# All values of thirteen pooled token tiles behind the routed experts, in four layouts of the pooled keys, and the residual loaded after the last tile

## The chip, the cores and the metric

The kernel runs on one core of a Trainium2 chip. The metric is the time of one execution in device microseconds (us); lower is better. A profiled execution also gives a span, from its first to its last instruction, which the views below are measured against.

## What is computed

The reference takes 2048 tokens of 512 numbers through two residual layers. Each layer normalises its input, computes a mixing branch `s` and a feed-forward branch, and adds `s * silu(ffn)` to the input:

```
xn = layernorm(x)
x  = x + rwkv(xn) * silu(moe2(xn))          # layer 0
xn = layernorm(x)
s  = attention(xn; 16 heads, 4 key heads)   # layer 1
g  = silu(shared_experts(xn) + routed_experts(xn))
x  = x + s * g
```

The change lies in layer 1. Its attention is over a short list of keys. The first 1792 tokens are pooled in blocks of 64 to 28 keys; only the last 256 tokens stay as single keys. A query sees a key if the key's position is not after its own. So a tile of 128 tokens, number `i` of 16, sees at most `2 * (i + 1)` pooled keys; tiles 0 to 13 see nothing but pooled keys, and tiles 14 and 15 are computed apart. The probabilities of one tile are 128 tokens x 16 heads x the keys, and the attention's result is their product with the values, multiplied by the output weights.

The feed-forward branch has two shared experts, which all tokens pass, and sixteen routed ones. Each token goes to four routed experts, weighted by a normalised gate.

## The kernel before

**Order of layer 1.** After the routing is known, the kernel computes keys and values, then tiles 14 and 15 of the attention (`full_group`), mixed with the shared experts of the last 512 tokens. It folds the query weights with the pooled keys into `sem` (lines 1515 to 1529), so that a tile's scores are one product with `xT`. The remaining shared experts follow (`hidden_shared`, line 972, and `down_shared`, line 1121); their result, with `acc`, is written by SP to two tables in main memory, `comb[0]` and `comb[1]`, one for each half of the 512 columns (line 1129).

**The routed loop.** Tokens are sorted by expert into tiles of 128 rows; there are 64 full ones' worth of rows and up to 80 tiles. `hidden_rows(j)` loads one expert's weights (line 674 to 678) and the tile's rows `x` (line 1674), turns the rows over (line 1681), and computes the hidden part (line 1688). `down_rows` computes the second product (line 1712), VectorE multiplies it with the gate (line 1717, four buffers of `y`), and GpSimd (POOL) sends it with an indirect transfer that adds each row to its token's row in both halves of `comb` (line 1720). Tiles from 65 on stand in a condition on the count of tiles; in the profiled execution 73 were needed, and seven conditions were passed by. An engine that passes one by still brings the semaphores to where they would have been.

**Attention inside the loop.** `attention()` is a generator. For each block of 256 tokens it projects the queries (two steps), computes scores and softmax of two tiles (`scores`, one step each, lines 1576 and 1582), and then, for tiles that are not in `LAST`, turns the probabilities over and multiplies them with the values (`turned` and `values`, lines 1608 and 1619). The loop takes a step every two tiles or so. A scheduler may place instructions ahead of where the program has them, when nothing holds them back; each engine then runs its own list strictly in order.

**Layouts of the pooled values.** With 32 keys for each head, four heads fill the 128 rows of a product, and a tile takes four products ("layouts" below). Tiles 1 to 7 see at most 16 keys. For these `vo8` holds the same values packed at 16 keys a head, and a tile takes two layouts. `vo8` is filled through main memory: `vo` is written to `vo_d` (line 1530), and SP loads 16 pieces of 16 rows from it (line 1534).

**The end.** The residual, `xr1`, was stored earlier. Its loads, `xo`, eight of 512 KB, are issued by SP inside the loop beside its last sixteen full tiles. After the loop `tiles.close()` gives the space of the weights, rows and `y` back. Then SP loads the sums from `comb` (line 1764, sixteen loads of 256 KB); PE computes the values of `LAST`, tiles 5 to 13; and `close` takes two tiles at a time: ScalarE's Silu on the sums (line 1772), VectorE's product with the attention's result (line 1774) and the addition of the residual (line 1778), and a store (line 1779). `pinned` keeps the Silus at their places in ScalarE's order: the first two stand behind the copy of tile 11's result.

Of the kernel before, what the change touches and what calls it, by code (L numbers as in the profile page):

```python
# [77 lines left out]
def tile_kernel(ctx: ExitStack, tc: tile.TileContext, a: dict):  # L78
# [1433 lines left out]
    vo8 = wq.tile([P, 2, D], F32, name="vo8")  # L1512
# [18 lines left out]
    for p in range(2):  # L1531
        for u in range(2):
            for j in range(4):
                nc.sync.dma_start(
                    out=vo8[(4 * u + j) * NARROW : (4 * u + j + 1) * NARROW, p, :],
                    in_=vo_d[j * KP : j * KP + NARROW, 2 * p + u, :],
                )

# [11 lines left out]
    fin = ctx.enter_context(tc.tile_pool(name="fin", bufs=NT // 2))  # L1550
# [6 lines left out]

    WIDE = NARROW * MB // P
    wide = [aq.tile([P, H, KP], F32, name=f"wide{i}") for i in range(WIDE, FULL[0])]
    near = [aq.tile([P, H, NARROW], F32, name=f"near{i}") for i in range(3)]  # L1560
    for t_ in (*wide, *near):
        nc.gpsimd.memset(t_, 0.0)

    def room_of(i):

        if i == 0:
            return aq.tile([P, H, KP], F32, tag="t1", name="all_keys"), KP
        nk = (i + 1) * P // MB
        return (near[i % 3] if i < WIDE else wide[i - WIDE]), nk
# [28 lines left out]
    def turned(i):  # L1598
# [3 lines left out]
        each = P // keys  # L1602
        nw = H // each
# [3 lines left out]
        for g in range(nw):  # L1607
            nc.tensor.transpose(
                pt[:, g, :], s[:, each * g : each * (g + 1), :].rearrange("p h k -> p (h k)"),
                ident,  # L1610
            )
        sT = aq2.tile([P, HKV, P], F32, tag="sT", name="sT")
        nc.scalar.copy(sT[:, 0:nw, :], pt)
        return i, nw, sT, vo if keys == KP else vo8
# [13 lines left out]
    LAST = range(5, FULL[0])  # L1628
# [106 lines left out]
    for j in range(NRT + 1):  # L1735

        with contextlib.ExitStack() as more:
# [9 lines left out]
            i = j - (FULL_TILES - NT)  # L1747
            if 0 <= i < NT and i % 2 == 0:
                xo = fin.tile([P, 2, D], F32, tag="xo", name="xo")
                nc.sync.dma_start(  # L1750
                    out=xo, in_=xr1[i * P : (i + 2) * P, :].rearrange("(n p) d -> p n d", p=P)
                )
                rest_of[i] = xo
# [3 lines left out]
    fin2 = ctx.enter_context(tc.tile_pool(name="fin2", bufs=NT // 2))  # L1757


    sums_of = {}  # L1760
    for i in range(0, NT, 2):
        y = fin2.tile([P, 2, D], F32, tag="y", name="y")
        for h, c_ in enumerate(comb):
            nc.sync.dma_start(
                out=y[:, :, h * D // 2 : (h + 1) * D // 2],
                in_=c_[i * P : (i + 2) * P, :].rearrange("(n p) d -> p n d", p=P),
            )
        sums_of[i] = y
# [123 lines left out]
```

## Time and profile before

| | |
|---|---|
| median of three runs | 1923.88 us (1922.08 to 1924.26) |
| profiled execution | time 1919.63 us, span 1917.9 us |
| last matmul of the shared experts ends | 1332.3 us |
| first product of the routed loop | 1340.29 us |
| first and last accumulating scatter start | 1347.20 and 1875.25 us |
| sums loaded from | 1883.65 us |
| VectorE's last stretch begins | 1895.27 us |

All times in the profile are microseconds from the start of the span. PE is TensorE's matmul, PEld its weight load, DVE VectorE, ACT ScalarE, POOL GpSimd, SP the engine that issues most transfers; SPq marks SP's issues. A line of the timeline has start, length, engine, source line, operation, output and inputs, and how many instructions were merged; in square brackets stands the idle time before it and what ended it. A line of the waits has who waited for whom, the total, how often, and the longest. The view by stretches gives, for a stretch of time, the busy time of each engine with its count, the granted clock of TensorE, the mean share of the 16 DMA engines and what they moved. A long share of busy time says that an engine was occupied, not that the end hangs on it.

### The profile page before, as it was taken

How to read it: one execution, taken by the hardware profiler on the slowest of the kernel's cores; microseconds unless marked ns; L12 is line 12 of the kernel's file. 1: busy time of each engine (PE TensorE's matmuls, PEld its weight loads, DVE VectorE, ACT ScalarE, POOL GpSimd, SP SyncE). 2: the span in 40 equal slices, each digit the busy share in tenths (PEclk: the TensorE clock that was granted, in tenths of full speed). 3: DMA queues.
4: the chain of work that ended last, by engine and by line, in shares of the span. 5: the costliest groups of instructions: out<-in, count | busy, mean ns of one | idle time of the engine just before them, and what ended most of it. 6: DMA issues, size and time to landing. Idle time of an engine off the chain costs nothing.

```text
span 1917.9 us, 23670 instructions
## 1 busy us (share of the span) xinstructions
PE 1848.1 (96%) x8107; PEld 1286.8 (67%) x8107; DVE 762.0 (40%) x1528; ACT 536.5 (28%) x1006; POOL 461.5 (24%) x349
## 2 busy tenths in 40 slices
PE   6999999999999999999989999999999999999996
PEld 4777777777877777777533654445767777777662
DVE  8354545272725435352166543421323223233313
ACT  6224232332423232332134112221222222222223
POOL 0211121120212111010210453000344444444341
PEclk9899999999999999999999999999999999999998
DMA  8657686635563434437461553122999999999896
GB/s 269 223 180 249 234 272 213 211 99 173 163 222 113 154 120 133 143 99 252 149 213 49 180 207 115 50 83 71 316 298 306 329 309 269 279 272 269 229 257 186
DMA packets 235989, 381.40 MB, mean 199 GB/s; under 512 B 19405, under 2 KB 136909, under 8 KB 234969
## 3 DMA queue, kind: packets, MB, share of 16 engines
q1 hardware_dynamic: 205784, 332.79, 52.3%
q0 software_dynamic: 28784, 45.63, 10.6%
q10 hardware_dynamic: 1296, 1.41, 0.3%
q8 instruction: 67, 1.10, 0.2%
q14 instruction: 58, 0.47, 0.1%
HBM read 294.04 MB, written 85.72 MB: 198 GB/s over the span
## 4 chain that ended last, share of the span: by engine, by line
PE 56%; DMA 6%; DVE 1%; issue 1%; ACT 1%; POOL 1%; SPq 0%; DVEq 0%; ACTq 0%; POOLq 0%
PE ph L1688 10%; PE py L1712 9%; PE pg L585 8%; PE py L607 4%; PE py L1121 4%; PE ph L972 3%; DMA comb<-y,to 3%; PE pq L1367 2%; PE proj L219 2%; PE po L727 2%; PE tp L1681 2%; PE ps L1576 1%; PE ps L1582 1%; PE pl L886 1%; PE pw L1492 1%
## 5 line engine op out<-in xcount | busy, mean ns | idle before, releaser
L585 PE MATMUL pg<-xg,w 128*128 128x256 f32 (+1 forms) x2304 | 494.9, 368 | 0.0
L585 PEld LDWEIGHTS pg<-xg,w 128*128 128x128 f32 x2304 | 419.5, 190 | 90.5 <-issue 42.3
L1720 POOL DMA_INDIRECT comb<-y,to x146 | 228.1, 1562 | 313.9 <-DMA comb<-y,to 183.4
L607 PE MATMUL py<-wd,hT 128*128 128x512 f32 x544 | 257.1, 593 | 3.5 <-DVE hT L592 3.5
L1688 PEld LDWEIGHTS ph<-xg,w 128*128 128x128 f32 (+1 forms) x1776 | 202.0, 182 | 40.4 <-ACT xg L1683 36.6
L1688 PE MATMUL ph<-xg,w 128*128 128x128 f32 (+1 forms) x1776 | 216.3, 278 | 0.7 <-issue 0.3
L592 DVE TENSOR_TENSOR hT<-sg,pg 128x256 f32<-128x256 f32 (+1 forms) x144 | 57.3, 402 | 380.4 <-ACT sg L590 380.2
L1712 PE MATMUL py<-w,ht 128*128 128x512 f32 (+1 forms) x438 | 207.8, 593 | 0.0
L590 ACT ACTIVATE sg<-pg 128x256 f32<-128x256 f32 (+1 forms) x144 | 53.0, 370 | 359.6 <-PE pg L585 359.3
L607 PEld LDWEIGHTS py<-wd,hT 128*128 128x128 f32 x544 | 102.2, 190 | 73.0 <-issue 61.9
L1717 DVE TENSOR_SCALAR y<-py,g 128x512 f32<-128x512 f32 x73 | 54.6, 748 | 219.7 <-PE py L1712 219.7
L958 ACT ACTIVATE ht<-ph,b1t 128x128 f32<-128x128 f32 (+1 forms) x222 | 81.2, 366 | 178.2 <-PE ph L1688 176.1
L1712 PEld LDWEIGHTS py<-w,ht 128*128 128x128 f32 (+1 forms) x438 | 75.9, 191 | 51.4 <-issue 45.2
L1683 ACT COPY xg<-tp 128x512 f32<-128x512 f32 x74 | 43.3, 585 | 186.9 <-PE tp L1681 186.9
L1121 PE MATMUL py<-w,hT 128*128 128x512 f32 (+1 forms) x192 | 89.4, 595 | 0.0
L972 PE MATMUL ph<-xT,w 128*128 128x512 f32 (+1 forms) x192 | 88.0, 597 | 0.0
L1059 POOL DMA_INDIRECT xs<-acc,slot x64 | 63.2, 987 | 66.0 <-DMA xs<-acc,slot 43.6
L267 POOL TENSOR_TENSOR ex<-st_p,qt 128x1024 f32<-128x1024 f32 x8 | 18.3, 2287 | 235.7 <-DVE qt L266 235.7
L727 PE MATMUL po<-wo,yb 128*128 128x512 f32 x128 | 57.4, 607 | 9.7 <-ACT acc L736 9.7
L1681 PEld LDWEIGHTS tp<-ident,x 128*128 128x128 f32 x296 | 36.9, 140 | 38.6 <-issue 20.8
L219 PE MATMUL proj<-xm,wr 128*128 128x256 f32 x256 | 61.5, 396 | 0.0
L219 PE MATMUL proj<-xm,wk 128*128 128x256 f32 x256 | 60.2, 389 | 0.0
(412 smaller groups left out, 2142.5 us busy)
## 6 DMA issues: line engine op xcount, KB each, us to landing
w<-in_w_dram SPq DMA_DIRECT2D x152, 352.0 KB
w<-in_w_dram SPq DMA_DIRECT2D x152, 256.0 KB
w<-in_w_gate_dram SPq DMA_DIRECT2D x72, 512.0 KB
w<-in_w_up_dram SPq DMA_DIRECT2D x72, 512.0 KB
wd<-in_w_down_dram SPq DMA_DIRECT2D x72, 512.0 KB
xs<-zero SPq DMA_DIRECT2D x16, 1360.0 KB
x<-xs SPq DMA_DIRECT2D x74, 272.0 KB
w<-in_w_dram SPq DMA_DIRECT2D x76, 192.0 KB
```

The source lines that it names most:

```text
L219: nc.tensor.matmul(out=ps[:, j, :], lhsT=w_[:, c, (o0 + j) * P : (o0 + j + 1) * P], rhs=xm[:, c, :], start=(c == 0), stop=(c == NC - 1),)
L585: nc.tensor.matmul(out=pg[:, i, 0:n], lhsT=w[:, c, i * FH + f * P : i * FH + (f + 1) * P], rhs=xg[:, c, 0:n], start=(c == 0), stop=(c == N ...
L607: nc.tensor.matmul(out=p, lhsT=hT[:, u * P : (u + 1) * P], rhs=wd[:, f, :], start=first_, stop=last_,)
L727: nc.tensor.matmul(out=po, lhsT=yb[:, c, s * P : (s + 1) * P], rhs=wo[:, c, :], start=(c == 0), stop=(c == NC - 1),)
L958: nc.scalar.activation(dst, src, AF.Relu, bias=b)
L972: nc.tensor.matmul(out=ph[0:n, :], lhsT=up(w, f, n, c), rhs=xT[:, c, cols], start=(c == 0), stop=(c == NC - 1),)
L1059: ins = nc.gpsimd.indirect_dma_start(out=xs, out_offset=bass.IndirectOffsetOnAxis(ap=slot[:, i, k : k + 1], axis=0), in_=acc[:, i, :], in_ ...
L1121: nc.tensor.matmul(out=py, lhsT=hT[0:n, e, f, s * P : (s + 1) * P], rhs=down(w, f, n), start=(e == 0 and f == 0), stop=(e == NS - 1 and f ...
L1681: nc.tensor.transpose(tp[:, c, :], x[:, c * P : (c + 1) * P], ident)
L1688: nc.tensor.matmul(out=ph[0:n, :], lhsT=up(w, f, n, c), rhs=xg[:, c, :], start=(c == 0), stop=(c == NC - 1),)
L1712: nc.tensor.matmul(out=py, lhsT=hT[0:n, f, :], rhs=down(w, f, n), start=(f == 0), stop=(f == NF1 - 1),)
L1720: nc.gpsimd.indirect_dma_start(out=c_, out_offset=bass.IndirectOffsetOnAxis(ap=to, axis=0), in_=y[:, h * D // 2 : (h + 1) * D // 2], in_of ...
```

## The change

- `LAST` grows from tiles 5 to 13 to tiles 1 to 13: only tile 0's values stay in the attention's steps. The steps in the loop go from 33 to 29.
- The values are packed at 8, 16, 24 and 32 keys for each head, and a tile takes the smallest that holds its keys: tiles 1 to 3 one layout of 128 rows, 4 to 7 two, 8 to 11 three, 12 and 13 four. Each tile 1 to 13 has its own buffer of probabilities, cleared by POOL (13 clears for 9).
- The packed values are loaded by ACT in fifty pieces of 8 to 24 rows, in place of SP's sixteen.
- The residual is loaded behind the loop in five loads (two of 512 KB, three of 1 MB), ahead of the sums; the sums come in ten loads in place of sixteen, of 256 or 512 KB each.
- The pairs of tiles are closed in the order of their numbers, pair 12 last.

```diff
-    vo8 = wq.tile([P, 2, D], F32, name="vo8")
+    by_keys = {k: wq.tile([P, H * k // P, D], F32, name=f"vo{k}") for k in (8, 16, 24)}
...
     nc.sync.dma_start(out=vo_d, in_=vo)
-    for p in range(2):
-        for u in range(2):
-            for j in range(4):
-                nc.sync.dma_start(
-                    out=vo8[(4 * u + j) * NARROW : (4 * u + j + 1) * NARROW, p, :],
-                    in_=vo_d[j * KP : j * KP + NARROW, 2 * p + u, :],
-                )
+    for k, rows_ in by_keys.items():
+        for h in range(H):
+            r0 = h * k
+            while r0 < (h + 1) * k:
+                r1 = min((h + 1) * k, r0 // P * P + P)
+                k0 = h % 4 * KP + r0 - h * k
+                nc.scalar.dma_start(
+                    out=rows_[r0 % P : r0 % P + r1 - r0, r0 // P, :],
+                    in_=vo_d[k0 : k0 + r1 - r0, h // 4, :],
+                )
+                r0 = r1
+    by_keys[KP] = vo
...
-    WIDE = NARROW * MB // P
-    wide = [aq.tile([P, H, KP], F32, name=f"wide{i}") for i in range(WIDE, FULL[0])]
-    near = [aq.tile([P, H, NARROW], F32, name=f"near{i}") for i in range(3)]
-    for t_ in (*wide, *near):
-        nc.gpsimd.memset(t_, 0.0)
+    probs = {}
+    for i in range(1, FULL[0]):
+        k = min(k for k in by_keys if k >= (i + 1) * P // MB)
+        probs[i] = aq.tile([P, H, k], F32, name=f"probs{i}")
+        nc.gpsimd.memset(probs[i], 0.0)
...
-        each = P // keys
-        nw = H // each
+        nw = H * keys // P
...
-    LAST = range(5, FULL[0])
+    LAST = range(1, FULL[0])
...
-            i = j - (FULL_TILES - NT)
-            if 0 <= i < NT and i % 2 == 0:
-                xo = fin.tile([P, 2, D], F32, tag="xo", name="xo")
-                nc.sync.dma_start(
-                    out=xo, in_=xr1[i * P : (i + 2) * P, :].rearrange("(n p) d -> p n d", p=P)
-                )
-                rest_of[i] = xo
...
     tiles.close()
-    fin2 = ctx.enter_context(tc.tile_pool(name="fin2", bufs=NT // 2))
+    fin = ctx.enter_context(tc.tile_pool(name="fin", bufs=1))
+    GROUPS = ((0, 2), (2, 2), (4, 4), (8, 4), (12, 4))
     sums_of = {}
-    for i in range(0, NT, 2):
-        y = fin2.tile([P, 2, D], F32, tag="y", name="y")
+    for i, n_ in GROUPS:
+        xo = fin.tile([P, n_, D], F32, name=f"xo{i}")
+        nc.sync.dma_start(
+            out=xo, in_=xr1[i * P : (i + n_) * P, :].rearrange("(n p) d -> p n d", p=P)
+        )
+        for k in range(0, n_, 2):
+            rest_of[i + k] = xo[:, k : k + 2, :]
+    for i, n_ in GROUPS:
+        y = fin.tile([P, n_, D], F32, name=f"y{i}")
         for h, c_ in enumerate(comb):
             nc.sync.dma_start(
                 out=y[:, :, h * D // 2 : (h + 1) * D // 2],
-                in_=c_[i * P : (i + 2) * P, :].rearrange("(n p) d -> p n d", p=P),
+                in_=c_[i * P : (i + n_) * P, :].rearrange("(n p) d -> p n d", p=P),
             )
-        sums_of[i] = y
+        for k in range(0, n_, 2):
+            sums_of[i + k] = y[:, k : k + 2, :]
...
-    closing = [i for i in range(0, NT, 2) if i < LAST[0] - 1]
-    closing += [i for i in (*range(0, NT, 2),) if i not in closing and i != FULL[0] - 2]
-    closing += [FULL[0] - 2]
+    closing = [i for i in range(0, NT, 2) if i != FULL[0] - 2] + [FULL[0] - 2]
```

More of the change, by code (lines that the diff above doesn't have):

```diff
@@ L1549, in tile_kernel @@
     aq2 = ctx.enter_context(tc.tile_pool(name="aq2", bufs=2))
-    fin = ctx.enter_context(tc.tile_pool(name="fin", bufs=NT // 2))
     tiles = ExitStack()
@@ L1567, in room_of @@
             return aq.tile([P, H, KP], F32, tag="t1", name="all_keys"), KP
-        nk = (i + 1) * P // MB
-        return (near[i % 3] if i < WIDE else wide[i - WIDE]), nk
+        return probs[i], (i + 1) * P // MB
     def scores(i, qg, u):
@@ L1608, in turned @@
             nc.tensor.transpose(
-                pt[:, g, :], s[:, each * g : each * (g + 1), :].rearrange("p h k -> p (h k)"),
-                ident,
+                pt[:, g, :], s.rearrange("p h k -> p (h k)")[:, g * P : (g + 1) * P], ident,
             )
@@ L1613, in turned @@
         nc.scalar.copy(sT[:, 0:nw, :], pt)
-        return i, nw, sT, vo if keys == KP else vo8
+        return i, nw, sT, by_keys[keys]
     def values(i, nw, sT, by_row):
```

## The prediction

> **What bounds the kernel now.** Start with the page: rows 1 and 2 give the engines' shares and the granted clock.
>
> ```profile
> PE 1848.1 (96%) x8107; PEld 1286.8 (67%) x8107; DVE 762.0 (40%) x1528; ACT 536.5 (28%) x1006; POOL 461.5 (24%) x349
> PE   6999999999999999999989999999999999999996
> PEclk9899999999999999999999999999999999999998
> DMA  8657686635563434437461553122999999999896
> ```
>
> TensorE is busy everywhere but at the two ends, at full clock. From slice 29 (1342 us), where the routed-expert loop begins, the DMA row is at 9 as well. So the change touches three stages with different limits: the shared experts (to 1332), the loop (1340 to 1867) and the end. The view by stretches separates them.
>
> ```profile
> 1340.00:1380.00 40.00, 39.47 (x217) 28.11 (x218) 10.86 (x30) 9.99 (x24) 12.61 (x9) 1.00 1.07 325
> 1380.00:1640.00 260.00, 259.85 (x1503) 192.04 (x1502) 74.65 (x254) 68.53 (x164) 114.66 (x74) 1.00 1.03 302
> 1640.00:1806.00 166.00, 165.97 (x906) 120.66 (x904) 55.28 (x164) 38.97 (x91) 66.30 (x43) 1.00 0.92 257
> 1806.00:1853.00 47.00, 47.00 (x271) 33.06 (x271) 10.79 (x43) 12.87 (x31) 19.05 (x12) 1.00 1.04 316
> 1857.00:1880.00 23.00, 18.59 (x70) 10.49 (x69) 0.75 (x1) 5.81 (x13) 12.40 (x8) 0.85 0.47 56
> ```
>
> After the length come the busy times of PE, PEld, DVE, ACT and POOL, then clock, DMA share, GB/s. PE is full in the loop, but so is something that no busy time shows: the accumulating scatters. For 1416 to 1640, the waits of POOL and the answer on line 1720 say:
>
> ```profile
> POOL comb L1720 <- DMA comb<-y,to: 110.8, 39, 6.7
> DMA to landing us min/median/max: 4.4/6.2/9.4
> ```
>
> Each tile adds its rows to both halves of `comb`, and a half's next scatter waits for the last to land. Tile 9's first scatter starts at 1416.58, tile 40's at 1636.82: 7.10 us a tile, nearly always ended by the landing of the one before. Two chains run abreast, PE's and this one. The end hangs on the second:
>
> ```profile
> SPq L1764 <- DMA comb<-y,to: 20.9, 1, 20.9
> L1737 POOLq INC_SWDGE_SEM x7: 847/857/891, 1875.3 to 1882.6; - x7
> 1883.65 9.90 SPq L1764 DMA_DIRECT2D y<-comb  x16
> 1892.88 1.28 ACT L1772 ACT_TABLE_LOAD   x1
> 1895.27 2.36 DVE L1774 TENSOR_TENSOR y<-xT,y 128x1024 f32<-128x1024 f32 x2 [34.17 <-DMA y<-comb]
> ```
>
> SP waits for the last scatter and for POOL's bookkeeping of seven skipped tiles behind it; the last tile's first scatter starts at 1873.40, and the sums are loaded from 1883.65. Call that moment T. Silu waits for ACT's turn (T+9.2), VectorE starts at T+11.6 and then never stops: 16 operations to 1913.52 (18.25 us), and the last store ends the span at 1917.9.
>
> **The change part by part.** Sums are against the profiled execution: span 1917.9, time 1919.63, which is 4.25 under the median of the three runs; I add the difference to the median.
>
> *Values out of the loop.* A wide tile of four layouts takes 3.87 us at the end (transposes at 1880.46 and 1884.34), 0.97 a layout. Before, tiles 1 to 4 cost two layouts each inside the loop: 8 x 0.97 = 7.8 us of PE. They go. The end had 3 x 2 + 6 x 4 = 30 layouts; it gets 3 x 1 + 4 x 2 + 4 x 3 + 2 x 4 = 31: +1.0 us of PE, which lies beside the loads at the end and costs nothing while these last longer (below).
>
> *Queries of the first block, ahead of the loop.* The built order puts the first block's 16 projections, both score tiles and tile 0's values before the first routed tile. SP's queue causes that: 16 loads of `vo8` (10.23 us from 1271.25 to 1281.48) no longer stand ahead of the cos/sin loads. PE work only moves (6.9 + 5.2 + 0.9 before line 1121's end, as 16 x 0.43, 4 x 0.86 + 4 x 0.43, and the small tile; PE was 100% busy in both places). But tile 0's values now wait for a copy between transposes and products: 0.58 us plus both hand-overs, about 0.9. And the first routed tile starts 13 us later, at about 1353.3 where it was 1340.29, so the first scatter goes from 1347.20 to about 1360.6.
>
> *Fifty loads on ACT.* They replace 16 on SP. Line 1534's issues have a median of 0.418 us, with the gap to the next 0.46; ACT's own constants at 1043 to 1044 go out at 0.4 to 0.5. So ACT issues for 50 x 0.46 = 23 us, behind it stand the four copies `wt`, `sem` and then every relu of the next shared block. The Trainium skill's "DMA: Bandwidth & Descriptors", section "Rules for kernel authors", speaks against it: coalesce many small transfers, "under 64 KB you're paying mostly overhead". These have 16 to 48 KB. If its section "Anatomy of one DMA" held with 2.0 us fixed for each in turn, it would be 100 us; the trace's 16 loads of 32 KB took 10.23 us together, so the pitch decides. I work ACT's end out: start 1271.3, 23 us of issue and 4.6 of copies would end at 1299, but the last four loads take semaphores used by the second block's cos/sin, whose buffer comes free only when VectorE has read the second projection (1305 + 0.7), plus 2.5 for that load: about 1310. PE has 6.9 us of shared hidden, 6.9 of projections and 6 of scores from 1291.1, to 1311, before it needs the first relu. Cost 0.4 us; bounds 0 and 10 (no cover at all from 1301 to 1311). POOL's 13 clears against 9 lie in an idle POOL.
>
> *Loop.* PE: -7.8 + 0.9 + 0.4 = -6.5. The scatters: until tile 12 the loop has almost no attention work, so tiles come at 5.8 us and DMA is full, as in the loop's first tiles, where the trace shows 7.8 us a scatter round (tile 1 at 1354.39, tile 9 at 1416.58). From 1360.6: 12 x 7.8 = 93.6, then 28 rounds at 7.1 and 22 at 6.9 (line 1720's median of 6.2 plus 0.7; 5.9 where less is moved) = 350.6: tile 62 at 1804.8. It was at 1806.43. The last ten rounds took 67.0 us to 1873.40 (no attention, DMA full, then empty) and will again. So T moves by 1804.8 - 1806.4 = -1.6 us, though PE has finished 6.5 earlier. Four buffers of `y` can hold the lag of some three tiles. Bounds: -6.5 (PE alone sets it) and +4 (7.2 a round in the middle).
>
> *The residual behind the loop.* Eight loads of 512 KB went out beside the last sixteen tiles, 4.2 MB hidden. Now five loads stand ahead of the sums on SP, in space that `tiles.close()` has to free: the built program puts the waits on all eight scatter semaphores on the first of them, and the first load of sums then has none left. They start at T, not earlier, and push the sums. The 16 sums took 15.0 us from 1883.65 to 1898.67 for the same 4.2 MB, at this rate in the middle:
>
> ```profile
> 1890.00:1894.00 4.00, 4.00 (x14) 2.04 (x13) 0.00 (x0) 1.70 (x2) 0.00 (x0) 1.00 1.09 358
> ```
>
> 4.19 MB at 358 GB/s are 11.7 us, so 3.3 is start and landing. The first pair's sum now lands at T + 3.3 + 11.7 + 1.5 = T+16.5. By the fit of "Anatomy of one DMA" (bytes at 436 GB/s) the residual would take 9.6, and the whole forecast would be 2.1 lower; the trace's 358 is taken. Behind the landing come the table load (1.28, now waiting for the sum) and one Silu (1.0): VectorE starts at T+18.8 instead of T+11.6. Later sums come every 1.5 us a pair, faster than VectorE's 2.27, so it stays the bound. Loss 7.2. That table load is a second place for the skill: "ScalarE: Activation LUTs", section "What ACT_TABLE_LOAD costs", gives 1283 ns and a drain of about 1380 for a switch; here the Silu starts at 1894.18, 0.02 after the load, so 1.28 is taken (with the drain, 1.4 more). Ten loads for sixteen save six times 0.46-0.6 of SP, hidden, since data is behind issue. PE ends its 31 layouts at about 1861 + 33 = 1894, and the last product waits for a copy that ACT does after two Silus, at T+20; VectorE needs it only at T+34. Hidden; without that cover, 3.6.
>
> Sum: -1.6 + 7.2 = +5.6. Span 1923.5; time 1923.88 + 5.6 = 1929.5.
>
> **The rivals.**
> 1. *PE alone sets the end.* If scatters catch up by tile 62 (in 1640 to 1806 they mostly waited for VectorE, not for a landing), T moves by -6.5: +0.7, time 1924.6. For it: that stretch. Against: the 7.10 us a tile before it, with PE's mean then only as fast.
> 2. *ACT's queue is not covered.* Loads that wait for each other's semaphores hold the relus, PE stalls in the shared block, up to 10 us: 1935 to 1939. For: ACT's last loads wait on VectorE's read of a projection. Against: 20 us of PE work stand before the need.
> 3. *Faster: the last ten scatter rounds.* They cost 67.0 us where PE needs 58 (ten tiles of 5.8). Seven of them run with DMA full, at a median landing of 6.8 (1820 to 1857); at 5.9, the median of 1640 to 1806, they would take 7 x 0.9 = 6 us less. With rival 1's -6.5 T moves by -12.5: net -5.3, time 1918.6. It decides at landings under 6.1 us there (net -3.9). Against: the residual was loaded before tile 62, so the change takes nothing from that stretch.
> 4. *The residual does not wait for the scatters* and lies beside POOL's 8 us of bookkeeping: no loss at the end, 1922.3 with my T. The built waits exclude it but for a misreading; under 0.01.
>
> **How the numbers follow.** What a measurement of this kernel can tell from no change is about 0.2%, 3.9 us. My forecast with its own spread (T from -5 to +3, end from 5.5 to 8): 0.55, of it 0.12 inside 3.9. Rival 1: 0.19, inside. Rival 2: 0.16, slower. Rival 3: 0.10, faster. So faster 0.10, same 0.31, slower 0.59. Time 1929.5; the forecast's own range is 1925 to 1935. The range that leaves out half of rival 3 and the upper half of rival 2: 1921 to 1937.
>
> **What would show it.** In the profile after: no `xo` load before T, five from T on, the first sum's wait behind them; VectorE's first product some 18 to 19 us after T; the loop's rounds at 7.0 to 7.2, last scatter near 1872; first routed tile near 1353; no PE idle over 1 us around 1300 to 1315; PE's last layout done before the first Silu. The forecast is wrong if VectorE starts under T+16, if the last scatter starts before 1868 or after 1877, or if PE stands in the shared block.

## The result, and the profile after

The changed kernel takes 1925.19 us in the median of 20 runs (1920.73 to 1930.69), the kernel before 1920.56 in 20 runs beside it (1917.81 to 1924.26). The ratio is 1.0019, 95% interval 1.0012 to 1.0025: slower by 3.7 us (2.3 to 4.8); it is not the quotient of the two medians, which are 4.6 us apart. A second set of 18 runs gave 1.0024 (1.0016 to 1.0032), 4.6 us. One run of 6621.61 us, of the kernel with the sums ahead of the residual, is left out of the ratios. The forecast was 5.6 us slower, from a base of 1923.88, which three runs had given; the sign was right, 1929.5 was 4.3 us too high, and 3.3 of these come from the base.

The profiled execution took 1920.73 us, its span is 1919.0. First rows 1 and 2 of its page.

```profile
PE 1843.1 (96%) x8086; PEld 1282.2 (67%) x8086; DVE 757.6 (39%) x1528; ACT 535.6 (28%) x1006; POOL 462.7 (24%) x353
...
PE   5899999999999999999989899999999999999995
...
DMA  8657686635563434437461553121999999999987
```

PE has 5 us less to do, and the span is no shorter. In the 31st slice (1439 to 1487 us) the digit stays at 9, yet the view by stretches shows a hole there. Its columns are as before: length, busy PE, PEld, DVE, ACT and POOL, clock, DMA share, GB/s.

```profile
1354.00:1380.00 26.00, 25.66 (x152) 18.73 (x151) 4.29 (x13) 6.28 (x17) 8.78 (x6) 1.00 1.07 326
1380.00:1460.00 80.00, 80.00 (x466) 57.68 (x464) 19.43 (x73) 21.15 (x51) 30.92 (x21) 1.00 1.08 332
1460.00:1480.00 20.00, 17.60 (x112) 13.19 (x111) 5.16 (x24) 5.42 (x14) 8.56 (x6) 1.00 0.92 269
1480.00:1640.00 160.00, 160.00 (x924) 119.27 (x923) 49.26 (x167) 39.04 (x93) 73.04 (x47) 1.00 1.00 285
1640.00:1801.00 161.00, 160.97 (x893) 117.52 (x893) 49.97 (x154) 38.98 (x92) 72.11 (x47) 1.00 0.97 271
```

Between 1460 and 1480 PE stands for 2.4 us, in a loop in which it never stood for more than 0.3 before. The timeline of VectorE, ScalarE and PE says why.

```profile
1473.26 0.75 DVE L1717 TENSOR_SCALAR y<-py,g 128x512 f32<-128x512 f32 x1 [4.83 <-DMA comb<-y,to]
1473.93 0.28 DVE L1594 TENSOR_TENSOR probs<-ps,n_pool 128x128 f32<-128x128 f32 x1
...
1474.89 0.31 ACT L1344 ACTIVATE probs<-probs 128x128 f32<-128x128 f32 x1 [4.73 <-DVE probs L1343]
1475.10 0.57 ACT L1683 COPY xg<-tp 128x512 f32<-128x512 f32 x1
...
1475.72 3.01 PE L1688 MATMUL ph<-xg,w 128*128 128x128 f32 x24 [2.08 <-ACT xg L1683]
```

Read from the top: VectorE waits 4.83 us to write a `y`, since the scatter that reads the old content of that buffer has not landed. Behind `y` in its queue stands the softmax of an attention tile, and it starts only when `y` is written. ScalarE's exponential waits for that, behind it in ScalarE's queue stands the copy `xg` of the next routed tile, and for `xg` PE waits. So the chain of scatters reaches PE through four buffers and two queues that have nothing to do with it. How far the scatters are behind can be read off for any tile: the second product of tile 14 and its first scatter.

```profile
1446.06 1.02 PE L1712 MATMUL py<-w,ht 97*128 97x512 f32 x2
...
1472.62 1.55 POOL L1720 DMA_INDIRECT comb<-y,to  x1 [3.78 <-DMA comb<-y,to]
```

The product ends at 1447.1, the scatter starts 25.5 us later; in the kernel before these two were 2.6 us apart. With a tile every 6.2 us 25 us are the four buffers of `y`. This distance is called the lag below.

The lag grows with the difference of two paces. Up to tile 12 PE makes a tile every 6.1 us and the scatters take 8.0 for one, so each tile adds 1.9 us to the 1.1 of tile 0, and at tile 12 the lag is 23.7. In the kernel before the scatters were hardly faster (7.7), but PE made a tile only every 7.5 us: from its first hidden product up to tile 13 it had 18.8 us of attention between the tiles, where it has 5.9 in the changed kernel.

Now the end: SP's waits from 1860 on, the answer on line 1737, and the timeline.

```profile
SPq L1757 <- DMA comb<-y,to: 19.8, 2, 18.7
```

```profile
L1737 POOLq INC_SWDGE_SEM  x7: 847/857/891, 1869.7 to 1876.9; - x7
```

```profile
1878.36 2.79 SPq L1757 DMA_DIRECT2D xo<-xr  x5
1881.19 15.67 SPq L1765 DMA_DIRECT2D y<-comb  x10
...
1894.06 1.28 ACT L1774 ACT_TABLE_LOAD   x1 [3.36 <-DMA y<-comb]
1895.36 2.00 ACT L1774 ACTIVATE y<-y 128x1024 f32<-128x1024 f32 x2
...
1896.45 2.36 DVE L1776 TENSOR_TENSOR y<-xT,y 128x1024 f32<-128x1024 f32 x2 [38.72 <-DMA y<-comb]
```

And the transfers' rate in the middle of the residual and the sums, from the view by stretches:

```profile
1890.00:1894.00 4.00, 3.95 (x13) 1.69 (x11) 0.00 (x0) 0.59 (x1) 0.00 (x0) 1.00 1.08 360
```

The first residual load waits for the scatters and the bookkeeping of seven skipped tiles, as the first load of sums did before. T is 1878.36 (1883.65 before), and ScalarE waits 3.36 us for the first sum. VectorE starts at T+18.1 (T+11.6 before) and ends 18.25 us later without a gap, as before.

Because the program ahead of the change is the same in all kernels here, and the issue of the first packed load nevertheless lies anywhere from 1270.8 to 1274.3 us among their profiles, stages are compared from that issue, called V. "PE" is the end of the last hidden product (line 1688 in the changed kernel), counted from V, and so is T, the first load behind the last scatter; VectorE's start and the end of the span are counted from T.

| profile | V | PE | T | VectorE starts | end |
|---|---|---|---|---|---|
| before | 1271.25 | 591.9 | 612.4 | T+11.6 | T+34.3 |
| after | 1271.75 | 588.0 | 606.6 | T+18.1 | T+40.7 |
| after, second profile | 1272.15 | 591.5 | 611.0 | T+18.5 | T+41.2 |

The two profiles of the changed kernel lie 4.9 us apart from V to the end. Every other run has one profile, so a difference of a few microseconds between two single profiles is weak evidence unless several kernels share it.

### The profile page after: what moved, and what is told of

Its sections match the earlier page's. It is cut to its first block, busy times and chain, and to the rows that moved or that the text cites. A ratio compares the mean times of both kernels' runs of the same rounds, so it can differ in the third digit from the quotient of the medians.

```text
span 1919.0 us, 23691 instructions
## 1 busy us (share of the span) xinstructions
PE 1843.1 (96%) x8086; PEld 1282.2 (67%) x8086; DVE 757.6 (39%) x1528; ACT 535.6 (28%) x1006; POOL 462.7 (24%) x353
## 4 chain that ended last, share of the span: by engine, by line
PE 52%; DMA 9%; DVE 2%; issue 1%; ACT 1%; SPq 1%; POOL 0%; DVEq 0%; ACTq 0%; POOLq 0%
PE pg L585 8%; PE ph L1688 8%; PE py L1712 8%; DMA comb<-y,to 5%; PE py L607 4%; PE py L1121 4%; PE ph L972 3%; PE pq L1367 2%; PE proj L219 2%; PE po L727 2%; PE ps L1578 1%; PE tp L1681 1%; DMA yg<-ys,slot 1%; PE pl L886 1%; PE pw L1492 1%
```

## The experiments

All ratios are to the kernel before on the same chip, with a 95% interval; 0.0010 is 1.9 us.

**The change again.** No edit.

> The changed kernel once more, for a second profile. Theory (the tail is fixed, the loop's accumulating scatters vary): the median is 1922 to 1928 us, VectorE's last stretch starts 18.1 us after the first load behind the last scatter (T), as in the first profile (1896.45 - 1878.36), and whatever the profiled time is above 1920.7 lies in T. Rival (the tail varies): T stays at 1878.4 and the distance from T to VectorE grows by what the time grows.

Ratio 1.0024 (1.0016 to 1.0032), median 1925.74. The profiled execution took 1926.10, 5.4 more than the first; 4.4 of it lie between V and T, 0.6 behind T. So the theory holds for these two profiles: what varies is the loop. The stall was worse this time (PE 4.3 us idle in the loop, 2.8 in the first profile), and it had a second part, in the timeline and in the view by stretches:

```profile
1464.69 4.38 PE L1688 MATMUL ph<-xg,w 128*128 128x128 f32 x24 [2.43 <-ACT xg L1683]
```

```profile
1464.60:1469.20 4.60, 4.51 (x25) 4.41 (x26) 0.43 (x3) 0.81 (x4) 0.54 (x2) 0.66 0.81 204
```

The 24 products behind the stall took 4.38 us, where they took 3.01 in the first profile: TensorE's clock was granted at 0.66 in these 4.6 us.

**The residual behind the loop, nothing else.** In the kernel before, the eight loads are taken out of the loop, and behind `tiles.close()` stands, ahead of the sixteen loads of sums:

```diff
-            i = j - (FULL_TILES - NT)
-            if 0 <= i < NT and i % 2 == 0:
-                xo = fin.tile([P, 2, D], F32, tag="xo", name="xo")
...
+    for i, n_ in GROUPS:
+        xo = fin.tile([P, n_, D], F32, name=f"xo{i}")
+        nc.sync.dma_start(
+            out=xo, in_=xr1[i * P : (i + n_) * P, :].rearrange("(n p) d -> p n d", p=P)
+        )
...
```

> The kernel before with one part of the change: the residual is loaded behind the loop in five loads ahead of the sums; values, layouts, packed loads and the sixteen loads of sums stay as before. Theory (this part alone costs what was lost): VectorE's last stretch starts 18 to 19 us after T where it started 11.6 after; T within 2 us of 1883.65; median 1920.6 + 6.5 = 1927, 1925 to 1929. Rival (eight loads of 512 KB beside the last sixteen tiles held up the scatters, so their leaving pays it back): the last ten rounds take 61 to 63 us in place of 67, T comes 4 to 6 us earlier, and the median is 1920 to 1923.

Ratio 1.0004 (0.9995 to 1.0012). Neither theory met what happened.

```profile
1869.68 2.96 SPq L1754 DMA_DIRECT2D xo<-xr  x5
1892.71 9.58 SPq L1765 DMA_DIRECT2D y<-comb  x16
```

In this kernel the residual goes out at 1869.68, before the last scatter (1882.6). Its first load waited 5.3 us for PE to pass the conditions and for no scatter, so its space seems not to be one that the scatters read; that is inferred from this wait. The loads lie beside the last scatters and hold them up: from 1869.6 to 1876 the transfers move 223 GB/s, where the kernel before moves 61 between 1869 and 1876, and the last round (the first scatters of tiles 71 and 72) takes 8.9 us in place of 4.6. All ten rounds from tile 62 on took 71.4 us in place of 67.0. T comes 6.4 us later, counted from V, and VectorE starts only 6.4 us after it. So this run doesn't price the change's order. It shows how much depends on what the loads have to wait for.

**The residual back in the loop.** In the changed kernel six of the eight loads stand in the loop of the program as before, and the last two pairs come in one load behind the sums.

```diff
+            i = j - (FULL_TILES - NT)
+            if 0 <= i < 12 and i % 2 == 0:
+                xo = finx.tile([P, 2, D], F32, tag="xo", name="xo")
...
-    for i, n_ in GROUPS:
-        xo = fin.tile([P, n_, D], F32, name=f"xo{i}")
...
         for k in range(0, n_, 2):
             sums_of[i + k] = y[:, k : k + 2, :]
+    xo = fin.tile([P, 4, D], F32, name="xo12")
...
```

> The changed kernel with the residual back in the loop: six of the eight pairs are loaded beside the last full tiles as before (more does not fit), the last two pairs (12 and 14) in one load behind the sums. Values of tiles 1 to 13 still stand last, in four layouts. Theory: VectorE starts 11.6 to 14.7 us after T (ScalarE reaches its first Silu only at T+12.3 in the profile of after, so the later end is likelier), and the median falls by 3.4 to 6.5 against the changed kernel: 1919 to 1922. Rival (values out of the loop and the later first scatter are themselves the loss): it stays at 1924 to 1926.

Ratio 0.9996 (0.9988 to 1.0005), as the theory wants. VectorE starts at T+13.4. T is at V+611.1 and PE at V+591.4, because in this build PE stands 4.7 us for the first rows ahead of the loop (the waits put it to `x<-xs`); the stall at 1460 to 1480 is gone.

Where these loads go out is not where the program has them. In this kernel all six are issued ahead of the loop, from 1277.2 to 1286.1. In the kernel before the eight were issued from 1431.37 on and the last at 1557.95, long before the last sixteen tiles:

```profile
1431.37 0.37 SPq L1750 DMA_DIRECT2D xo<-xr  x1
```

So this run, and those below with part of the residual in the loop, show what it is worth to have these bytes loaded before T. They don't show what the loads would cost beside the last tiles.

**Sums ahead of the residual, group by group.**

```diff
     for i, n_ in GROUPS:
         y = fin.tile([P, n_, D], F32, name=f"y{i}")
...
         for k in range(0, n_, 2):
             sums_of[i + k] = y[:, k : k + 2, :]
+        xo = fin.tile([P, n_, D], F32, name=f"xo{i}")
+        nc.sync.dma_start(
+            out=xo, in_=xr1[i * P : (i + n_) * P, :].rearrange("(n p) d -> p n d", p=P)
+        )
```

> The changed kernel with one thing different: each group's sums are loaded ahead of the same group's residual (sums 0, residual 0, sums 2, residual 2, and so on), in place of all residuals ahead of all sums. Loop and values are unchanged. Theory: the first sum lands at about T+5, but ScalarE is through with tile 11's copy only at T+12.3; with the table load and a Silu VectorE starts at T+14.7 in place of T+18.1, later sums and residuals arrive at 358 GB/s (all 8.4 MB by T+27) ahead of its need: 3.4 us gained, median 1921 to 1922. Rival 1 (the first pair's sum is not what VectorE waits for): no gain, 1925. Rival 2 (the alternating order starves VectorE, gaps of over 1 us between its operations): gain under 1.5 us.

Ratio 1.0013 (1.0005 to 1.0022), 1 to 2 us less than the change where the theory asked for 3.4; the intervals overlap. VectorE starts at T+12.5 in place of T+18.1, but the span ends at T+38.1 in place of T+40.7: of 5.6 us gained at the start 2.6 are left at the end. VectorE works 18.25 us without a gap here too, but the last store ends 7.4 us behind it (4.3 in the change). With 4.2 MB of sums, 4.2 of residual and 4.2 of stores all behind T, the transfers become the bound; at 358 GB/s they need 35 us, an estimate. PE stalls in the loop here too, 4.0 us.

**The packed loads on SP.**

```diff
-                nc.scalar.dma_start(
+                nc.sync.dma_start(
                     out=rows_[r0 % P : r0 % P + r1 - r0, r0 // P, :],
```

> The changed kernel with the fifty loads of packed values issued by SP in place of ScalarE. They then stand ahead of the cos/sin loads again, so that the first block's queries and scores fall back into the loop's first tiles as in the kernel before; the rest of the change stays. In the two profiles of the changed kernel PE stands 3.5 and 5.1 us in the loop, mostly at 1460 to 1480, where ScalarE's xg copy stood behind a softmax that VectorE was late with, VectorE itself standing at a y whose buffer the scatters had not freed. Theory (taking the attention out of the first twelve tiles makes them outrun the scatters): PE's idle time in the loop is under 1 us, the last hidden product ends some 584 us after the first packed load is issued, where it ended 588.0 and 591.4 after it (before: 591.8), and the median falls by 2 to 4: 1921 to 1923.5. Rival (the stall is chance, the order does not matter, and SP's 23 us of issue delay the weights): no gain or a loss, 1925 to 1930.

Ratio 0.9989 (0.9981 to 0.9998): 6 us less than the change, and a little less than the kernel before. PE's waits in the loop, 1340 to 1860:

```profile
PE ph L1688 <- issue: 0.3, 1, 0.3
PE pw L1619 <- ACT sT L1613: 0.2, 1, 0.2
```

And its timeline at the end:

```profile
1873.79 2.57 SPq L1757 DMA_DIRECT2D xo<-xr  x5
...
1892.48 2.36 DVE L1776 TENSOR_TENSOR y<-xT,y 128x1024 f32<-128x1024 f32 x2 [39.48 <-ACT y L1774]
```

The stall is gone, PE is at V+584.2 as expected, 7.7 us before the kernel before: the eight layouts. T is at V+603.0, 9.4 earlier. VectorE starts at T+18.7. This is the change without the early attention (the first block's queries and scores and tile 0's values ahead of the loop), and it shows the prediction's two large terms bare: 7.7 us gained in the loop (7.8 forecast), 7.1 lost between T and VectorE's start (7.2 forecast; 7.7 up to the end of the span). All five kernels with the packed loads on SP have PE at V+583.6 to 585.2; the three profiles with the early attention and no remedy, two of the changed kernel and one with the sums ahead of the residual, have it at 588.0 to 591.5.

**Eight buffers of `y`.**

```diff
-        to = m1x.tile([P, 1], I32, tag="to", bufs=6, name="to")
+        to = m1x.tile([P, 1], I32, tag="to", bufs=10, name="to")
...
-        y = m1x.tile([P, D], F32, tag="y", bufs=4, name="y")
+        y = m1x.tile([P, D], F32, tag="y", bufs=8, name="y")
```

> The changed kernel with eight buffers of y in place of four (and ten of the scatter's indices in place of six); every engine's list of instructions is the same. Theory: the stall of PE at 1460 to 1480 comes through y, so its idle time in the loop falls from 3.5 to 5.1 us to about 1 and the last hidden product ends 3 to 4 us earlier. If the end hangs on PE there, the median falls by 3 to 4, to 1921.5 to 1922.5; if the chain of scatters sets the end all the same, only PE is earlier and T stays, 1924.5 to 1926. Rival (the stall comes from the weights' or rows' loads): PE's idle time stays at 3.5 to 5.

Ratio 1.0008 (1.0002 to 1.0014), 2 to 3 us less than the change. In the loop there is one wait of PE left:

```profile
PE ph L1688 <- DMA w<-in_w_dram: 0.8, 1, 0.8
```

With the order of PE's, VectorE's, ScalarE's and POOL's instructions unchanged, buffers alone take the stall away. The scatter's indices `to` have more of them too, but it is `y` that VectorE waited to write in the changed kernel. PE is at V+586.0, T at V+605.2, 19.2 behind it (18.6 and 19.5 in the change): T comes forward with PE. The scatters still lag, by 28 us at tile 20, but PE no longer feels it.

**A second pair of tables for the odd tiles.** Nothing reads the second pair, so the sums lack the odd tiles' rows; the kernel is there for its time alone.

```diff
-        for h, c_ in enumerate(comb):
+        for h, c_ in enumerate(comb if j % 2 == 0 else comb_odd):
```

> The changed kernel with the routed tiles of odd number added into a second pair of tables, which nothing reads: the sums lack the rows of those tiles. A table's next scatter then waits for the one two tiles before, so the chain of landings is cut in two. Theory (the chain of landings bounds the front of the loop and the last ten rounds): the first twelve rounds take under 7 us each in place of 8.0, PE's stall at 1460 to 1480 goes, the last ten tiles take about 58 us in place of 64.5 to 65.4, and T comes 4 to 8 us earlier: 1918 to 1921.5. Rival (the transfers' bandwidth bounds both, the landings only get longer): rounds stay within 0.3 us of the changed kernel's, 1924 to 1927.

Ratio 0.9973 (0.9963 to 0.9984), 9 to 10 us less than the change. What POOL's scatters waited for from the first to tile 62, the changed kernel (first line) and this one (the others), as total, times, longest:

```profile
POOL comb L1720 <- DMA comb<-y,to: 170.9, 72, 5.5
```

```profile
POOL comb_odd L1721 <- DMA comb<-y,to: 4.3, 3, 3.7
POOL comb L1721 <- DMA comb_odd<-y,to: 3.6, 5, 2.4
```

The wait for landings has gone, the lag is 1.1 us at nearly every tile, the first twelve rounds take 6.1 us each (8.0 in the change), the last ten 54.7 us (64.5). T is at V+594.4, 12.2 us earlier than in the first profile of the change, but the end only 7.4: VectorE starts at T+23.0, as ScalarE's first Silu now stands behind the copy of tile 11's values (1887.26) and no longer waits for the loads. With as many bytes scattered: it is the wait of one scatter for the landing of the one before, not bandwidth, that makes the rounds.

**A mix for the end.** Five residual loads in the loop of the program (issued at 1275.8 to 1284.8, ahead of it), three behind the sums, six buffers of `y` and eight of `to`, and the pairs closed from tile 9 on. Of the edit the last part:

```diff
-        if i >= LAST[-1] - 2:
-            for _ in range(2):
-                close(closing.pop(0))
+        for _ in range({9: 2, 10: 1, 11: 1, 12: 2}.get(i, 0)):
+            close(closing.pop(0))
```

> The changed kernel with six buffers of y, five of eight residual pairs loaded in the loop as before, the other three behind the sums, and the pairs closed from tile 9 on (two at tile 9, one each at 10 and 11, two at 12) in place of from tile 11 on. Theory: the tail has only 4.2 + 1.6 MB to load, the first sum lands at about T+5, and ScalarE reaches its first Silu at about T+6.5, so VectorE starts at T+8.5 to T+10 in place of T+18.1; with T unchanged or 3 us earlier the median falls by 8 to 12, to 1913 to 1917. As in the kernel with the residual in the loop, the scores of the second tile fall back into the loop, and PE may again wait some 5 us for the first rows before the loop (1350): then 1916 to 1919. Rival (the transfers bound the tail: 4.2 + 1.6 + 4.2 MB of store at 358 GB/s are 28 us): the end is not before T+33, a gain of some 6 us and no more.

Ratio 0.9985 (0.9978 to 0.9992), some 7 us less than the change; VectorE starts at T+10.2, the end is at T+33.2. Here too PE stands some 5 us for the first rows, and PE is only at V+592.8. The gain is near the rival's.

**The same mix, with the packed loads on SP.** The edit above, and

```diff
-                nc.scalar.dma_start(
+                nc.sync.dma_start(
                     out=rows_[r0 % P : r0 % P + r1 - r0, r0 // P, :],
```

> The changed kernel with the fifty packed loads on SP, six buffers of y, five residual pairs in the loop and three behind the sums, and the pairs closed from tile 9 on (two at tile 9, one each at 10 and 11, two at 12). Theory: PE loses its 7.7 us of values in the loop with no new stall (as with the loads on SP alone: last hidden product 584 us after the first packed load), T about 603 after it, and the tail is that of the mixed kernel, 33.2 us from T to the end in place of 42.0: 0.44% below the kernel with the loads on SP alone, so 0.9945 to 0.996 of the kernel before. Rival (the residual in the loop lengthens the scatter rounds, T comes later by 3 to 5): 0.997 to 0.9985.

Ratio 0.9943 (0.9930 to 0.9956), from five runs: 11 us below the kernel before, 8.8 by the two medians (1909.59 and 1918.38), the best of all.

```profile
1878.84 7.74 SPq L1766 DMA_DIRECT2D y<-comb  x10
1886.62 2.90 SPq L1774 DMA_DIRECT2D xo<-xr  x3
...
1886.34 2.36 DVE L1783 TENSOR_TENSOR y<-xT,y 128x1024 f32<-128x1024 f32 x2 [29.33 <-ACT y L1781]
```

VectorE starts at T+7.5 and the span ends at T+31.0, with T at V+605.0.

**Sums first and early closes, all residual behind the loop, packed loads on SP.** Three edits shown above together: `nc.sync` for the packed loads, each group's `xo` behind its `y`, and the earlier `close`.

> The changed kernel with the fifty packed loads on SP, all of the residual behind the loop but each group's sums ahead of its residual, and the pairs closed from tile 9 on. Theory (the transfers bound such a tail: 4.2 MB of sums, 4.2 of residual, 4.2 of stores at 358 GB/s are 35 us, 38 with start and landing, wherever VectorE starts): T at 603 after the first packed load, the end 38 after T where it is 42 with all residuals first; 2 to 4 us less than the kernel with the loads on SP alone, 0.997 to 0.998 of the kernel before. Rival (VectorE's start decides): VectorE starts at T+9 to T+10 in place of T+18.7 and the whole 9 us are gained, 0.994 to 0.995.

Ratio 0.9977 (0.9966 to 0.9987). VectorE starts at T+6.0, stands 4.8 us between its operations, and the end is at T+37.7. So the theory holds: with all of the residual behind T the transfers bound the end though VectorE starts early. No run with all of the residual behind T, in any order, got below T+37.7; those with most of it loaded before T did (T+31.0 to T+36.0).

**The residual in the loop, packed loads on SP.** Two edits shown above together: `nc.sync` for the packed loads, and `if 0 <= i < 12` in the loop with the last two pairs behind the sums; the closes are as in the change.

> The changed kernel with the fifty packed loads on SP and the residual in the loop for six of eight pairs, the last two behind the sums; y keeps four buffers, the pairs are closed from tile 11 on as in the change. Beside the kernel with the loads on SP alone only the residual's place differs. Theory (the residual ahead of the sums costs what the prediction says, less what ScalarE's turn leaves): VectorE starts at T+13 to T+14 in place of T+18.7, and the median is 4 to 6 us lower, 0.996 to 0.997 of the kernel before. Rival (the residual's loads in the loop hold up the scatters by as much): within 1.5 us of it, 0.998 to 0.9995.

Ratio 0.9961 (0.9949 to 0.9974), from five runs, against 0.9989 for the packed loads on SP alone: 5.4 us by the two ratios, 3.5 by the quotients of the medians. VectorE starts at T+12.4, the end is at T+34.8 where it is T+42.0; T itself is 2.2 us later. The six loads go out at 1299.2 to 1325.8, ahead of the loop. This is the price of the residual's place with the rest of the change kept: some 7 us behind T, 5 net from V to the end.

**The early attention alone, in the kernel before.**

```diff
-    pending, taken = None, 0
+    for _ in range(5):
+        next(attend)
+    pending, taken = None, 5
```

> The kernel before with one thing different: the first five steps of the attention (queries of the first block, scores of tiles 0 and 1, values of tile 0) are taken ahead of the first routed tile, and no attention step follows until the tile at which the sixth was due. Work is the same, only its order. Theory (the early attention is what keeps the first tiles from outrunning the scatters): the scatter of tile 14 starts 20 us or more behind its second product (2.6 us in the kernel before), PE stands 3 to 6 us in the loop near tiles 16 to 20, and the median rises by 3 to 6 us, 1.0015 to 1.003. Rival (order does not matter for the end, the scatters catch up): within 1.5 us, 0.999 to 1.0008.

Ratio 0.9998 (0.9989 to 1.0007). The theory fell. The lag does rise, to 15 us at tile 10 and 18 at tile 28, but not to 25: PE stands 0.7 us in the loop. PE's pace is as in the change (6.2 us a tile up to tile 12), but the scatters need only 7.4 in place of 8.0. Early attention that stands behind the shared experts, as here, is not what costs.

**What else the stall needs.** Two more runs asked this. In the first, the kernel with the packed loads on SP gets the same edit. In the second, the changed kernel is as it was but for

```diff
-            if taken < PARTS and (j + 1) * PARTS // FULL_TILES > taken:
+            if taken < PARTS and (j + 6) * PARTS // FULL_TILES > taken:
```

> The changed kernel with the fifty packed loads on SP and, as in the kernel before with the early attention, the first five attention steps taken between the last shared product and the first routed tile; no attention step follows until the tile at which the sixth is due, 13. Theory A (where the early attention stands decides: behind the shared products it gives the first weights 14 us of head start, ahead of them none, since their space is not free yet): first scatter near 1361, the scatter of tile 14 at most 18 us behind its product, PE's idle in the loop under 1.5 us, 0.998 to 0.9997 of the kernel before (the loads on SP alone: 0.9989). Theory B (the values taken out and the attention's late return decide, wherever the early steps stand): the lag reaches 24 us, PE stands 3 to 5 us at tiles 16 to 20, 1.0003 to 1.002.

> The changed kernel with one number different: each attention step is due five tiles earlier, so that the second block's steps begin at tile 8 in place of 13; the early attention still stands ahead of the last shared products. Theory B (the long stretch of routed tiles without attention lets PE outrun the scatters): the lag stays under 20 us, PE's idle in the loop falls from 3.5 to 5.1 us to under 1.5, 0.9998 to 1.0012 of the kernel before in place of 1.0019 and 1.0024. Theory A (the cold start of the transfers decides): the first rounds stay at 8.0 us, the lag and PE's stall only move, 1.0015 to 1.003.

The first has a ratio of 1.0006 (0.9993 to 1.0019), an interval that takes in both theories. Its trace speaks for theory A: the lag does not exceed 18.5 us (tile 20), PE stands 0.7 us in the loop, T is at V+603.7 as with the packed loads on SP alone. The scatters take 7.4 us a tile up to tile 12, as in the run before this one, at the same pace of PE (6.1). A difference that may explain it stands in the stretch just before the routed loop, first of the changed kernel, then of this one:

```profile
1340.00:1347.00 7.00, 7.00 (x20) 3.15 (x18) 0.88 (x2) 0.00 (x0) 0.08 (x1) 1.00 0.11 37
```

```profile
1340.00:1347.00 7.00, 7.00 (x34) 4.86 (x33) 2.92 (x7) 0.00 (x0) 0.00 (x0) 1.00 0.97 318
```

In both PE is full, but in the changed kernel it is busy with the last shared products and the transfers are nearly idle at 37 GB/s, while here it does the attention and the first weights come in at 318. The weights' space is opened behind the shared experts (`sh.close()`); that it is this which holds the loads back is read from the code, not shown by a run. The changed kernel enters its loop with little loaded ahead, and moves 332 GB/s without a pause until 1460.

The second has 1.0022 (1.0013 to 1.0032), no gain. By its trace theory B is right on the stall: lag 18.9 at most in the first twenty tiles, PE idle 0.3 us, PE at V+584.7. The first rounds stay at 8.0 us and the ratio is in theory A's range. By the clock the edit bought nothing: the attention is now used up five tiles earlier, PE runs through the tiles behind it at 5.8 us each, and the scatter of tile 62 is 7.7 us behind its product where it is 1.6 or 1.7 in the kernel before, in the changed one and in all others. T is at V+608.9, 24 us behind PE; in the changed kernel it is 19 behind. The stall was moved to the end of the loop and turned into a wait for scatters.

So either remedy keeps the lag under four buffers, and the changed kernel has neither: its transfers start late, and no step of the attention is due until tile 13 (only projections of the next block, placed early, stand between the tiles). How many microseconds each of them gives is not settled, the interval of the first being too wide.

## Why the prediction was right or wrong

| from the kernel before | forecast | first and second profile |
|---|---|---|
| PE, from V | -6.5 | -3.9 and -0.4 |
| T, from V | -1.6 | -5.8 and -1.4 |
| VectorE's start, from T | +7.2 | +6.5 and +6.9 |
| end of the span, from V | +5.6 | +0.6 and +5.5 |
| time | +5.6 | +3.7 and +4.6 (by ratio) |

Two steps on the loop failed, and with opposite signs: T follows PE and not the scatters, which brings it forward, and PE stands in the loop, which sends it back. What they left together is close to rival 1's +0.7 in the first profile (+0.6) and to the forecast's +5.6 in the second (+5.5). That the sum came near is luck; the part behind T is not.

*The base.* The forecast added 5.6 to the median of three runs, 1923.88. Twenty runs of the same kernel have a median of 1920.56, fifty-five later ones 1921.49. Of the 4.3 us by which 1929.5 was missed, 3.3 are this; the prediction saw that its profile lay 4.25 under the median and still took the median.

*Values out of the loop: right.* 7.8 forecast, 7.7 measured with the packed loads on SP.

*The residual ahead of the sums: right, slightly over.* 7.2 forecast, 6.5 and 6.9 measured in the changed kernel, 7.1 with the loads on SP. The rate taken from the trace (358) showed up again (360 GB/s from 1890 to 1894); with 436 from the Trainium skill's "DMA: Bandwidth & Descriptors", section "Anatomy of one DMA", a fit that it gives for transfers issued by GpSimd while SP issued these, the term would have been 5.1. The Silu started 0.02 us after its table load again. All five loads left behind the last scatter, as the prediction said, and the rival that denied it is dead for this kernel. In the kernel before with the residual behind the loop that rival's case did occur, and it saved nothing there, since the loads met the last scatters. The eight loads of the kernel before did not go out beside the last sixteen tiles, as the prediction has it, but between 1431 and 1558.

*"The end hangs on the second", the chain of scatters: the step that failed.* The prediction took the scatters' waits for each other (110.8 us from 1416 to 1640) as a sign that they, and not PE, lead up to tile 62, and so let T move by -1.6 only. A wait for the landing before says that the rounds fill their time, not that they are behind. Two lines of the chain that ended last in the kernel before, with the scatter of tile 62 between them, show who led:

```profile
1802.26 2.58 PE py L1712 x6
...
1806.43 1.97 POOL L1720 DMA_INDIRECT comb<-y,to  x1 [6.81 <-DVE mx L1348]
...
1829.86 6.14 DMA comb<-y,to
```

The second product of tile 62 ends at 1804.84 and its scatter starts 1.6 us later. In the kernel before the lag is never over 5.8 us up to there, and its chain goes through PE until 1825.3 and only then through scatters. In the changed kernel the scatter of tile 62 started at 1803.3, near the 1804.8 forecast, but 1.7 us behind its product: the chain had caught up, as rival 1 said. T follows PE through tile 62 plus ten rounds of 64.5 to 65.4 us (67.0 forecast). Where PE gained 7.7 us (packed loads on SP) T came 9.4 earlier, where it gained 5.9 (eight buffers) 7.2. The forecast's -1.6 for T lies in the measured span of -5.8 to -1.4, for another reason: PE lost what it should have gained.

*"PE work only moves": the other step that failed.* The early attention was priced at 0.9 us. It left the first thirteen tiles nearly bare, the scatter rounds there took 8.0 us (8.3 in the second profile), and four buffers of `y`, which the prediction took to be enough, filled up. Its own figures said so: 7.8 us a round less 5.8 a tile, over twelve tiles, is a lag of 24 us, four tiles of some 6 us and not the three that it let the buffers hold. PE lost 2.8 and 4.3 us in the loop standing (0.7 before), and in the second profile some more at a lowered clock. That is the larger part of what PE did not gain: with eight buffers PE is at V+586.0, 5.9 us ahead of the kernel before, near the forecast's 6.5. The prediction's explanation of the early attention (SP's queue) is supported: with the fifty loads on SP it goes away.

*Fifty loads on ACT: priced right, as a queue.* ScalarE was free at 1310.0 as worked out, and PE never stood in the shared block. On SP the fifty went out in 22.8 us, the 0.46 each that was worked out. What the term left out is that the queue which takes them decides where the attention is placed, and that was worth 6 us between two kernels. No run had fewer, larger loads, so whether coalescing them helps stays open.

*What was to show the forecast wrong.* VectorE started later than T+16, and PE did not stand in the shared block. The last tile's first scatter started at 1867.8, just outside the 1868 to 1877 given, its second at 1869.6; in the second profile the first started at 1872.6.

## What to carry to other kernels

Two chains that run abreast with few buffers between them are priced by the lag, not by the mean pace: read the distance from producer to consumer tile by tile, and compare it with buffers times pace. That one chain waits for its own landings doesn't make it the one that leads; a short lag says that it only keeps up. Before taking work out of such a loop, ask what that work was spacing: with attention between the tiles the scatters' 7 us were hidden, without it they showed up as a stall in front, or as a wait at the end. And behind the last dependence of this kernel the bytes to be loaded decided when VectorE could start; move those that do not depend on it ahead of it, and read in the trace when they really go out, since the place in the program doesn't tell.

## What the runs showed of the hardware

A short stall costs PE more than its length, at times. Behind 2.43 us of standing the next 24 products took 4.38 us at a granted clock of 0.66, behind 2.08 us 3.01 us at 1.00; in the kernel with the sums first 4.46 us behind 1.83, at 0.77 in the 3 us from 1479 on. So it isn't the length alone that decides. The Trainium skill's "TensorE: Matmul & The Clock Gate", section "Part 1: The HAM clock gate", describes a free-running window of about 3.4 us of activity, which would make the outcome depend on where the stall falls; these stalls were shorter than it, and no run here shows the window itself.

The accumulating scatters at the front of this loop are bound by waiting, not by bytes: with two tables taking turns the same rows went through at 6.1 us a tile in place of 8.0, with POOL's instructions at the same 1.55 us each.
